# Head sums behind the first value product, division and factor sums moved into the next even step

## The chip, the cores and the metric

The kernel runs on one core of one Trainium2 chip, as one program with one launch. The metric is the device time in microseconds (us). TensorE does the matmuls and has a separate record for the loading of its stationary operand ("weight load", PEld in the profile). VectorE (DVE), ScalarE (ACT) and GpSimd (POOL) do the elementwise work, SyncE (SP) issues most transfers. Each engine works through its own queue in order, and waits on semaphores for the others.

## The reference

The input x has 4 sequences of 512 rows with 512 features. It is normalised, and the result is x plus an attention plus a mixture of expert networks, both of the normalised rows. All is float32. The change touches the attention alone. Its core, cut:

```python
scores = jnp.einsum('bhqd,bhkd->bhqk', q, k)          # 16 heads; 128 + 64 (rotary) features
scores = jnp.clip(scores, -80.0, 80.0)
causal = pos[:, None] >= pos[None, :]
scores = jnp.where(causal[None, None], scores, -jnp.inf)
weights = jax.nn.softmax(scores / jnp.sqrt(jnp.float32(d_qk)), axis=-1)
attn = jnp.einsum('bhqk,bhkd->bhqd', weights, v)
out = attn.transpose(0, 2, 1, 3).reshape(B, S, H * D_H) @ W_O.T
```

The softmax is split up in the kernel: exponentials first, the product with the values with them, and the division by their sum only on the product's result. No maximum is taken, since the clip bounds the scores.

## The kernel before

The first half of the program (to about 657 us) normalises, routes the rows and runs the experts; the experts' results lie in device memory (`y_d`), to be added later. The second half is the attention, a loop over 32 steps; step i works on one pair of heads of one sequence (4 sequences times 8 pairs). Everything in it is float32.

In step i:

- `scores` makes the scores of both heads of pair i in TensorE: eight matmuls from the plain features (L1432) and eight from the rotary ones (L1443). They lie in PSUM banks named a0, a1 (key block 0), c and a rotating one (block 2), b0 and b1 (blocks 1 and 3).
- `weights` lets VectorE clip them out of PSUM into `pt` (L1461, six operations), ScalarE take the exponentials (L1465), and GpSimd zero the upper triangles (L1469, eight masks). GpSimd then adds up the exponentials over the key blocks into `su`, one tile per head (L1493, L1497). A clip is what frees a score bank.
- For pair i + 1, TensorE makes the queries (L1282, L1297); VectorE turns the rotary ones with five operations (L1268, L1271), and GpSimd ends that with a subtraction (L1272). In the code this is `turn_q`.
- `values(i - 1, j)` multiplies the previous pair's exponentials with the values (L1513), and ScalarE copies the result into `og`, one tile for two pairs, that is for four heads.

Two pairs, four heads, form a group q, closed in an even step. The group's division has these parts:

- `sums(q)`: four matmuls of `su` with ones, 32 columns each, into one bank, and that bank is a0, the one that the scores use as well (L1532). VectorE takes the reciprocal `rc` (L1534).
- `spread_by_dma(q, rc)`: 16 small transfers on SyncE's queue copy the rows of `rc` to all partitions (`rb`, L1544).
- `divide(q)`: four VectorE multiplications of `og` by `rb` (L1566), then four additions and subtractions (L1572, L1575) that make the left factors for a Strassen-like product of seven block products instead of eight.
- `project_out(q)`: the seven block products with the output weights (L230, 56 matmuls) in banks b1, c and b0. ScalarE copies some results out (L1605), GpSimd adds these to the accumulator `acc` (L1612), and VectorE adds the rest straight from the banks (L1615, three operations; the last two free b0 and b1). In between `combine` adds the experts' rows of one of 16 row groups to `acc` with three VectorE operations (L1677), and `fetch` gathers the next three tiles of such rows by indirect transfers that GpSimd issues (L1664).

`project_out(q - 1)` is called in the even step after the one that made `sums(q - 1)`. So before the change the sums of group q come in even step i = 2q + 2, the division of group q in the odd step i + 1, and its projection in the even step i + 2.

Most instructions are recorded with `keep`, which holds them in the program's order on their engine. The indirect transfers and the GpSimd additions between them are placed by the scheduler.

Of the kernel before, what the change touches and what calls it, by code (L numbers as in the profile page):

```python
# [10 lines left out]
F32 = mybir.dt.float32  # L11
# [7 lines left out]
P = 128  # L19
B, S, D = 4, 512, 512  # L20
# [22 lines left out]
def kernel(  # L43
# [164 lines left out]
    def first_factors(add, sub, a11, a12, a21, a22, s1, s2, s4, s3):  # L208
        add(s1, a21, a22)
        sub(s2, s1, a11)  # L210
        sub(s4, a12, s2)
        sub(s3, a11, a21)
        return a11, a12, s4, a22, s1, s2, s3
# [998 lines left out]
    def lat(b, i):  # L1212
        return xnT[:, i, ts(b, S)]

    def project(b, psum):

        if b % 2 == 0:
            two = psum(f"pj_kr_{b}")
            for c in range(DC):
                for j in range(2):  # L1220
                    r = slice(j * DHR, (j + 1) * DHR)
                    keep(
                        nc.tensor.matmul(
                            two[r, :],
                            krT[:, c, r],
                            xnT[:, c, ts(b + j, S)],
                            start=(c == 0),
                            stop=(c == DC - 1),
                        )
                    )  # L1230
            raw = hw.tile([P, S], F32, tag="raw", name=f"kraw_{b}")
            keep(nc.scalar.copy(raw, two))
            turned[b] = hw.tile([P, S], F32, tag="kr", name=f"kr_{b}", bufs=1)
            rope(turned[b], raw, f"k{b}")
        ps = []
        for wT, name in ((dqT, "cq"), (dkvT, "ckv")):
            p = psum(f"pj_{name}_{b}")
            for c in range(DC):
                keep(
                    nc.tensor.matmul(  # L1240
                        p, wT[:, c, :], xnT[:, c, ts(b, S)], start=(c == 0), stop=(c == DC - 1)
                    )
                )
            ps.append(p)
        keep(nc.scalar.copy(lat(b, 0), ps[0]))
        keep(nc.vector.tensor_copy(lat(b, 1), ps[1]))

        src = turned[b - b % 2][(b % 2) * DHR : (b % 2 + 1) * DHR, :]
        for j in range(2):
            keep(nc.vector.tensor_copy(lat(b, 2)[j * DHR : (j + 1) * DHR, :], src))  # L1250
# [29 lines left out]
    def rotary_query(i, ps):  # L1280
        b, hp = pairs[i]
        keep(nc.tensor.matmul(ps, qrT[:, hp, :], lat(b, 0), start=True, stop=True))  # L1282
        raw = hw.tile([P, S], F32, tag="raw", name=f"qraw_{i}")
        qr = hw.tile([P, S], F32, tag="qr", name=f"qr_{i}", bufs=1)
        qs[i] = [qr]

        def copy():
            keep(nc.scalar.copy(raw, ps))

        def turn():  # L1290
            rope(qr, raw, f"q{i}")

        return copy, turn

    def query(i, j, ps):
        b, hp = pairs[i]
        keep(nc.tensor.matmul(ps, a_h[:, 2 * hp + j, :], lat(b, 0), start=True, stop=True))  # L1297
        qc = hw.tile([P, S], F32, tag=f"qc{j}", name=f"qc_{i}_{j}", bufs=1)
        qs[i].append(qc)

        def copy():
            keep(nc.scalar.copy(qc, ps))

        return copy
# [96 lines left out]
    ap = ctx.enter_context(tc.tile_pool(name="ap", bufs=2))  # L1401
# [4 lines left out]
    def psum(name):  # L1406
        return ps_p.tile([P, S], F32, tag="pj", name=name)
# [6 lines left out]
    def scores(i):  # L1414
        b = pairs[i][0]
        qr, *qc = qs.pop(i)
        bank = {}
        for j in range(2):
            bank[j, 0] = ps_s.tile([P, S], F32, tag=f"a{j}", name=f"sa_{i}_{j}")
            bank[j, 1] = bank[j, 3] = ps_s.tile([P, S], F32, tag=f"b{j}", name=f"sb_{i}_{j}")  # L1420
        bank[0, 2] = ps_s.tile([P, S], F32, tag="c", name=f"sc_{i}")
        bank[1, 2] = psum(f"sd_{i}")

        def where(j, kc):
            o = 3 * P if kc == 3 else 0
            return bank[j, kc][:, o : o + PT_W[kc]]

        order = [(j, kc) for kc in (0, 2, 1, 3) for j in range(2)]
        for j, kc in order:

            keep(
                nc.tensor.matmul(  # L1432
                    where(j, kc),
                    lat(b, 1)[:, ts(kc, P)],
                    qc[j][:, kc * P :],
                    start=(kc != 3),
                    stop=False,
                )
            )
        for j, kc in order:  # L1440
            r = slice(j * DHR, (j + 1) * DHR)
            keep(
                nc.tensor.matmul(  # L1443
                    where(j, kc),
                    lat(b, 2)[r, ts(kc, P)],
                    qr[r, kc * P :],
                    start=False,
                    stop=(kc != 1),
                )
            )  # L1450
        return bank
# [54 lines left out]
    def values(i, j):  # L1506

        b, q = pairs[i][0], i // 2
        pt = pts[i]
        av = psum(f"av_{i}_{j}")  # L1510
        for kc in range(TPB):
            keep(
                nc.tensor.matmul(  # L1513
                    av[:, kc * P :],
                    lat(b, 3)[:, ts(kc, P)],
                    pt[:, PT[j, kc] : PT[j, kc] + PT_W[kc]],
                    start=(kc == 0),
                    stop=(kc == TPB - 1),
                )
            )  # L1520
        if q not in og:
            og[q] = ap.tile([P, 4, S], F32, tag="og", name=f"og_{q}")
        keep(nc.scalar.copy(og[q][:, 2 * (i % 2) + j, :], av))

    def bank(tag):
        return lambda name: ps_s.tile([P, S], F32, tag=tag, name=name)

    def sums(q):

        sb = bank("a0")(f"sb_{q}")  # L1530
        for j, su in enumerate(sus.pop(2 * q) + sus.pop(2 * q + 1)):
            keep(nc.tensor.matmul(sb[ts(j, 32), :], ones[:, :32], su, start=True, stop=True))  # L1532
        rc = ap.tile([P, S], F32, tag="rc", name=f"rc_{q}", bufs=1)
        keep(nc.vector.reciprocal(rc, sb))  # L1534
        return rc
# [3 lines left out]
    def spread_by_dma(q, rc):  # L1539
        spread[q] = []  # L1540
        for j in range(4):
            rb = ap.tile([P, S], F32, tag="rb", name=f"rb_{q}_{j}", bufs=4)
            for m in range(4):
                nc.sync.dma_start(rb[ts(m, 32), :], rc[ts(j, 32), :])  # L1544
            spread[q].append(rb)
# [11 lines left out]
    def divide(q):  # L1557

        o = og.pop(q)

        for cols in half if q == n // 2 - 1 else [slice(0, S)]:
            for j, rb in enumerate(spread[q]):
                keep(nc.vector.tensor_mul(o[:, j, cols], o[:, j, cols], rb[:, cols]))  # L1566
        a11, a21 = (o[:, 0:2, half[t]] for t in range(2))
        a12, a22 = (o[:, 2:4, half[t]] for t in range(2))
        x = [ap.tile([P, 2, S // 2], F32, tag=f"s{k}", name=f"s{k}_{q}") for k in (1, 2, 4)]

        def add(*t):
            keep(nc.vector.tensor_add(*t))  # L1572

        def sub(*t):
            keep(nc.vector.tensor_sub(*t))  # L1575

        firsts_of[q] = first_factors(add, sub, a11, a12, a21, a22, *x, a21)
# [109 lines left out]
    for i in range(n):  # L1687
        more = i + 1 < n
        even = i % 2 == 0
        q = i // 2 - 1  # L1690
        held = scores(i)
        raw_copy, turn_q = rotary_query(i + 1, psum(f"pqr_{i + 1}")) if more else (nothing, nothing)
        qc_copy = query(i + 1, 0, psum(f"pq_{i + 1}_0")) if more else nothing
        weights(i, held, raw_copy, nothing if even else turn_q)
        qc_copy()
        if even and i > 0:
            spread_by_dma(q, sums(q))
        if even:
            turn_q()
        if i > 0:  # L1700
            values(i - 1, 0)
        if more:
            query(i + 1, 1, psum(f"pq_{i + 1}_1"))()
        if i < 2:
            project(2 + i, psum)
        if 1 < i < 5:
            turn_keys((2, 3, 1)[i - 2], psum)
        if i > 0:
            values(i - 1, 1)
        if even and i > 2:  # L1710
            project_out(q - 1, first_added=lambda: combine(q))
        if i == 1:
            combine(0)
        if even and i != 2 or i == 1:
            fetch((i + 1) // 2)
        if not even and i > 1:
            divide(q)

    q = n // 2 - 1

# [59 lines left out]
```

## Time and profile before

| | |
|---|---|
| median of 14 runs | 1340.21 us (1339.92 to 1341.24) |
| the profiled execution | 1340.78 us |
| its span, first to last instruction | 1339.0 us |
| busy: TensorE / weight loads / VectorE / ScalarE / GpSimd | 99 / 74 / 73 / 30 / 63% of the span |
| mean granted TensorE clock | 0.999 |
| first score matmul of step 0, step 31 | 657.39 us, 1291.85 us |
| reciprocal L1534 | 16 times, 3.35 us each |
| division's multiplications L1566 | 68 times, 68.6 us in all, median 0.77 us |
| clips L1461 into the rows of `sa` | 64 times, 0.68 us each |
| masks L1469 | 256 times, 0.57 us each on average |

A line of the timeline gives the start in us from the span's start, the busy time of the merged group in us, engine, source line, operation, output and input by name, shapes and count; in square brackets stands how long the engine was idle before it and what ended that. A line of the waits gives the waiting engine, tile and line, what released it, the total in us, how many times, and the longest. Matmuls overlap, so a group's start-to-next-start distance says more than its busy time. Each float32 matmul appears as two records.

### The profile page before, as it was taken

The numbers are of one execution on the slowest core, as the hardware profiler recorded it, in microseconds if no ns is written. First come the engines' busy times: TensorE is split into PE (matmuls) and PEld (weight loads), VectorE is DVE, ScalarE is ACT, GpSimd is POOL, SyncE is SP. The second block draws the span as 40 slices with busy tenths as digits, with TensorE's granted clock in tenths as the row PEclk, the third lists the DMA queues.
The fourth block names the chain that finished last, engine by engine and source line by source line (L and its number), as shares of the span: only waits on it lengthen the run. The fifth ranks groups of instructions, "written<-read, shape, count | busy, mean of one in ns | idle before, by whom it ended". The sixth has DMA issues, their size and how long they took to land.

```text
span 1339.0 us, 17913 instructions
## 1 busy us (share of the span) xinstructions
PE 1329.6 (99%) x5949; PEld 992.7 (74%) x5949; DVE 971.6 (73%) x1426; ACT 406.3 (30%) x714; POOL 847.7 (63%) x952
## 2 busy tenths in 40 slices
PE   9999999999999999999999999999999999999998
PEld 8778888888888888877655666666666666666676
DVE  7669486676767677676458679877788777897775
ACT  3333222322223322212223423323333323233231
POOL 5113664564545465532277789888898888988883
PEclk9999999999999999999999999999999999999999
DMA  8850355766567675533401331243322333213332
GB/s 280 192 158 19 92 134 159 219 180 185 185 169 204 164 228 162 156 92 99 142 21 46 111 109 37 85 132 110 110 56 73 124 111 110 82 53 118 110 110 87
DMA packets 174100, 167.90 MB, mean 125 GB/s; under 512 B 57904, under 2 KB 136752, under 8 KB 174000
## 3 DMA queue, kind: packets, MB, share of 16 engines
q1 hardware_dynamic: 161264, 133.10, 33.9%
q0 software_dynamic: 12736, 33.57, 8.6%
q8 instruction: 49, 0.80, 0.3%
q14 instruction: 51, 0.42, 0.1%
HBM read 116.02 MB, written 34.87 MB: 113 GB/s over the span
## 4 chain that ended last, share of the span: by engine, by line
PE 96%; DVE 2%; DMA 1%; SPq 1%; ACT 1%; issue 0%; POOL 0%; DVEq 0%; ACTq 0%; POOLq 0%
PE op L230 14%; PE av L1513 11%; PE yr L230 11%; PE hr L230 10%; PE gr L230 9%; PE sb L1432 4%; PE sa L1432 4%; PE pq L1297 4%; PE gs L230 3%; PE sa L1443 3%; PE ys L230 2%; PE pqr L1282 2%; PE hs L230 2%; PE sb L1443 2%; PE sb L1532 2%; PE h_s L142 1%
## 5 line engine op out<-in xcount | busy, mean ns | idle before, releaser
L182 POOL DMA_INDIRECT xs<-xn_d,idx_i x208 | 230.0, 1106 | 193.6 <-DVE xT L199 134.6
L1469 POOL TENSOR_TENSOR pt<-pt,tri 128x128 f32<-128x128 f32 x256 | 140.1, 567 | 68.4 <-ACT pt L1465 61.7
L1465 ACT ACTIVATE pt<-pt 128x512 f32<-128x512 f32 x160 | 94.4, 628 | 257.6 <-DVE pt L1461 256.6
L1513 PEld LDWEIGHTS av<-pt,xnT 128*128 128x128 f32 x512 | 95.4, 190 | 83.7 <-issue 47.7
L1513 PE MATMUL av<-pt,xnT 128*128 128x512 f32 (+3 forms) x512 | 149.8, 436 | 0.0
L230 PE MATMUL op<-m,og 128*128 128x256 f32 x512 | 118.6, 379 | 0.5 <-DVE og L1566 0.5
L1271 DVE TENSOR_TENSOR swap_q<-qraw,sinT 32x512 f32<-32x512 f32 x128 | 117.7, 919 | 1.7
L1497 POOL TENSOR_TENSOR su<-su,pt 128x256 f32<-128x256 f32 (+1 forms) x128 | 105.2, 822 | 10.0
L230 PEld LDWEIGHTS op<-m,og 128*128 128x128 f32 x512 | 96.0, 190 | 14.5 <-DVE og L1566 1.3
L1461 DVE TENSOR_SCALAR pt<-sa 128x512 f32<-128x512 f32 x64 | 41.1, 682 | 70.2 <-PE sa L1443 70.2
L1664 POOL DMA_INDIRECT yg<-y_d,pos_i x48 | 54.5, 1134 | 57.1 <-issue 50.2
L230 PE MATMUL op<-m,s 128*128 128x256 f32 x384 | 88.2, 379 | 0.1
L1497 POOL TENSOR_TENSOR su<-pt 128x384 f32<-128x384 f32 x64 | 83.8, 1310 | 0.0
L1612 POOL TENSOR_TENSOR acc<-acc,v 128x512 f32<-128x512 f32 x60 | 80.6, 1344 | 5.1 <-ACT v L1605 3.2
L230 PEld LDWEIGHTS op<-m,s 128*128 128x128 f32 x384 | 72.9, 190 | 10.3 <-issue 0.5
L1677 DVE SCALAR_TENSOR_TENSOR acc<-yg,wk,acc 128x512 f32<-128x512 f32 x48 | 56.7, 1181 | 19.1 <-POOL acc L1612 17.9
L1605 ACT COPY v<-op 128x512 f32<-128x512 f32 x64 | 37.5, 587 | 108.3 <-PE op L230 107.1
L1566 DVE TENSOR_TENSOR og<-og,rb 128x512 f32<-128x512 f32 (+1 forms) x68 | 68.6, 1069 | 0.6 <-PE rb L1552 0.2
L230 PE MATMUL yr<-w,at_r 128*128 128x256 f32 x288 | 67.1, 380 | 0.7 <-DVE at_r L351 0.4
L1615 DVE TENSOR_TENSOR acc<-op,acc 128x512 f32<-128x512 f32 x48 | 31.7, 687 | 49.5 <-POOL acc L1612 47.3
L230 PE MATMUL hr<-xT,w 128*128 128x256 f32 x288 | 66.1, 379 | 0.0
L230 PE MATMUL gr<-xT,w 128*128 128x256 f32 x288 | 66.1, 379 | 0.0
(339 smaller groups left out, 2809.2 us busy)
## 6 DMA issues: line engine op xcount, KB each, us to landing
m<-m_d SPq DMA_DIRECT2D x112, 256.0 KB
w<-in_L_ffn_W_dram SPq DMA_DIRECT2D x52, 512.0 KB
rb<-rc SPq DMA_DIRECT2D x240, 64.0 KB
w<-in_L_ffn_Wg_dram SPq DMA_DIRECT2D x26, 512.0 KB
y_d<-v_yr SPq DMA_DIRECT2D x36, 256.0 KB
y_d<-none SPq DMA_DIRECT2D x24, 256.0 KB
acc<-in_L_attn_x_dram SPq DMA_DIRECT2D x16, 256.0 KB
xn_d<-xp SPq DMA_DIRECT2D x16, 256.0 KB
```

The costliest lines, as they stand in the source:

```text
L182: nc.gpsimd.indirect_dma_start(out=xs[blk][:, q, :], out_offset=None, in_=xn_d[:, :], in_offset=bass.IndirectOffsetOnAxis(ap=idx_i[:, q, b ...
L230: nc.tensor.matmul(banks[k][:, t, :], a[p][:, j, ts(t, P)], b[p][:, j, :], start=(k not in used), stop=(t == j == 1), skip_group_check=True,)
L1271: keep(nc.vector.tensor_mul(swap[there, :], raw[here, :], tables[1][here, :]))
L1432: nc.tensor.matmul(where(j, kc), lat(b, 1)[:, ts(kc, P)], qc[j][:, kc * P :], start=(kc != 3), stop=False,)
L1443: nc.tensor.matmul(where(j, kc), lat(b, 2)[r, ts(kc, P)], qr[r, kc * P :], start=False, stop=(kc != 1),)
L1465: keep(nc.scalar.activation(t, t, AF.Exp, scale=QK_SCALE))
L1469: keep(nc.gpsimd.tensor_mul(m, m, tri))
L1497: nc.gpsimd.tensor_add(t[:, kc * P :], prev, pt[:, PT[j, kc] : PT[j, kc] + PT_W[kc]])
L1513: nc.tensor.matmul(av[:, kc * P :], lat(b, 3)[:, ts(kc, P)], pt[:, PT[j, kc] : PT[j, kc] + PT_W[kc]], start=(kc == 0), stop=(kc == TPB - 1),)
L1566: keep(nc.vector.tensor_mul(o[:, j, cols], o[:, j, cols], rb[:, cols]))
L1612: keep(eng.tensor_add(block, block, v))
L1677: nc.vector.scalar_tensor_tensor(acc[:, g, :], yg, wk[:, g, k : k + 1], acc[:, g, :], ALU.mult, ALU.add)
```

## The change

Three places of the attention loop change.

1. In an even step, `spread_by_dma(q, sums(q))` is called after `values(i - 1, 0)` instead of before it. On TensorE the four sum matmuls move behind eight value records; on VectorE the reciprocal moves behind the turn of the queries, since `turn_q` is called before.
2. `divide` is no longer called at the end of the odd step. Group q - 1 is divided in the next even step, behind the clips of `weights` and ahead of the turn; `project_out(q - 1)` follows later in the same step. The group left over at the end of the loop is divided right after it, which is the place where it was divided before.
3. The three tiles of the factor sums (`s1`, `s2`, `s4`) have one buffer each instead of two.

```diff
-        x = [ap.tile([P, 2, S // 2], F32, tag=f"s{k}", name=f"s{k}_{q}") for k in (1, 2, 4)]
+        x = []
+        for k in (1, 2, 4):
+            x.append(ap.tile([P, 2, S // 2], F32, tag=f"s{k}", name=f"s{k}_{q}", bufs=1))
...
         weights(i, held, raw_copy, nothing if even else turn_q)
         qc_copy()
-        if even and i > 0:
-            spread_by_dma(q, sums(q))
+        if even and i > 2:
+            divide(q - 1)
         if even:
             turn_q()
         if i > 0:
             values(i - 1, 0)
+        if even and i > 0:
+            spread_by_dma(q, sums(q))
         if more:
...
-        if not even and i > 1:
-            divide(q)
+    divide(q)
```

In the program's order VectorE's queue in an even step becomes: six clips, four multiplications and four factor sums of the division, five operations of the turn, the reciprocal, one bank addition, three operations of the combine, two bank additions. In an odd step it holds six clips and five operations of the turn. GpSimd's queue keeps its operations; in most even steps its second `acc` addition now stands ahead of the first two gather issues, in steps 4, 12, 20 and 28 it stands behind them, as it did before in every even step.

## The prediction

> **What bounds it now.** I read the busy shares, then the chain, then what the weight loads wait for (TensorE's own rows name no such wait), then the timeline of a pair of steps. The page:
>
> ```profile
> PE 1329.6 (99%) x5949; PEld 992.7 (74%) x5949; DVE 971.6 (73%) x1426; ACT 406.3 (30%) x714; POOL 847.7 (63%) x952
> ...
> PE 96%; DVE 2%; DMA 1%; SPq 1%; ACT 1%; issue 0%; POOL 0%; DVEq 0%; ACTq 0%; POOLq 0%
> ```
>
> TensorE is the chain. But a busy matmul row can hide a weight load that waits. The waits of the weight loads, 720 to 1290 us:
>
> ```profile
> PEld sb L1532 <- DVE pt L1461: 10.7, 14, 0.8
> PEld sb L1532 <- POOL su L1497: 4.4, 13, 0.4
> ```
>
> So the sums of four heads (L1532) come too early in each even step: their bank a0 is freed by a clip that stands behind the division, and the fourth `su` is late on GpSimd. The price is in TensorE's timeline; step 12 first, then the last sums, where nothing is late:
>
> ```profile
> 901.62 1.53 PE L1532 MATMUL sb<-su,ones 128*32 128x512 f32 x8
> 903.08 2.42 PE L1513 MATMUL av<-pt,xnT 128*128 128x512 f32 x8
> ...
> 923.03 1.90 PE L1432 MATMUL sb<-qc,xnT 128*128 128x384 f32 x8
> ```
> ```profile
> 1314.35 1.07 PE L1532 MATMUL sb<-su,ones 128*32 128x512 f32 x8
> ...
> 1315.35 1.99 PE L230 MATMUL op<-m,og 128*128 128x256 f32 x8
> ```
>
> From start to next start the sums take 1.46 us in step 12 and 1.00 at the end. By the first score matmuls (851.56, 879.18, 892.94, 920.45 ...) an even step lasts 27.51 us and an odd one 13.76, from step 5 to the end. VectorE and GpSimd in step 12 (one answer for each engine), where the combine waits for GpSimd's first addition:
>
> ```profile
> 900.86 1.28 DVE L1461 TENSOR_SCALAR pt<-sa 128x512 f32<-128x512 f32 x2
> ...
> 903.91 3.35 DVE L1534 RECIPROCAL rc<-sb 128x512 f32<-128x512 f32 x1
> 907.17 0.81 DVE L1268 TENSOR_TENSOR qr<-qraw,cosT 128x512 f32<-128x512 f32 x1
> 907.99 4.08 DVE L1271 TENSOR_TENSOR swap_q<-qraw,sinT 32x512 f32<-32x512 f32 x4
> 912.10 0.69 DVE L1615 TENSOR_TENSOR acc<-op,acc 128x512 f32<-128x512 f32 x1
> 915.68 2.33 DVE L1677 SCALAR_TENSOR_TENSOR acc<-yg,wk,acc 128x512 f32<-128x512 f32 x3 [2.88 <-POOL acc L1612]
> 920.82 1.29 DVE L1615 TENSOR_TENSOR acc<-op,acc 128x512 f32<-128x512 f32 x2 [2.82 <-POOL acc L1612]
> ```
> ```profile
> 914.38 1.27 POOL L1612 TENSOR_TENSOR acc<-acc,v 128x512 f32<-128x512 f32 x1
> 916.71 1.47 POOL L1664 DMA_INDIRECT yg<-y_d,pos_i  x1 [1.06 <-DVE acc L1677]
> 918.48 1.01 POOL L1664 DMA_INDIRECT yg<-y_d,pos_i  x1 [0.30 <-issue]
> 919.51 1.27 POOL L1612 TENSOR_TENSOR acc<-acc,v 128x512 f32<-128x512 f32 x1
> ```
>
> The last two additions free banks b0 and b1; the score matmul at 923.03 writes b0. VectorE has 1.5 us in hand there and 5.7 us of waits before, but no more. And step 31, the one place where the division already stands straight behind the clips:
>
> ```profile
> 1297.42 1.29 DVE L1461 TENSOR_SCALAR pt<-sa 128x512 f32<-128x512 f32 x2 [4.02 <-PE sa L1443]
> ...
> 1300.49 3.27 DVE L1566 TENSOR_TENSOR og<-og,rb 128x512 f32<-128x512 f32 x4
> ...
> 1306.13 1.48 DVE L1575 TENSOR_TENSOR og<-og 128x512 f32<-128x512 f32 x1
> ```
>
> **Sums behind the values.** No instruction is added. The clips now start when the scores are done, the fourth `su` has 2 us more, and the sums should take 1.00 us in place of 1.46. Step 4 has no such wait today (736.45 to 737.46). Saved: 0.46 x 13 even steps (6 to 30) = 6.0 us. Bounds: 0 if `su` stays late, 0.6 at most. The `su` buffers and a0 are held about 2 us longer; GpSimd's next `su` comes after its eight masks, later than that, so I price this at nothing.
>
> **Division into the even step.** Eight VectorE operations leave the odd step, where they take 8.5 us (851.09 to 859.59) and VectorE then has room, and enter the even step. I count from the first score matmul (0). Clips start at 5.57, the division at 8.64 and ends at 15.76 (step 31: 1291.85, 1297.42, 1300.49, 1307.61). The projection needs its first input at about 15 and s2 at about 18.7, so it doesn't wait.
>
> The five operations of the turn follow. The nearest row is 4.9 us (907.17 to 912.07); beside masks it was 4.5. GpSimd has 3.0 us of `su` work left at that point (0.59 + 0.45 + 0.29 + 0.99 + 0.72, step 31's rows), and the two engines alternate: a mask lasts 0.455 alone and 0.90 beside these operations, one each 0.86, so a VectorE operation holds GpSimd for 0.41. 3.0 + 5 x 0.41 = 5.1; it ends at 20.9. The reciprocal, now behind the turn, takes 3.26: 24.1. Bank addition 0.65: 24.8.
>
> Ten steps (6, 8, 10, 14, ...): the combine touches other rows than GpSimd's first addition and goes on at once. In step 10 it took 4.38 (three GpSimd operations beside it), alone 2.33; with two beside it I take 4.1: 28.9. Then 0.69 and 0.61: b0 free at 29.6, b1 at 30.2. The score matmuls want them at 27.51 - 0.46 + 2.58 = 29.63 and 30.28. That is no margin at all: I take 0.1 us of wait per step, between 0 and 0.5. 1.0 us.
>
> Four steps (4, 12, 20, 28; the combine's group lies in the block of the first addition): combine waits for that addition, GpSimd's second addition stands behind two gather issues that wait for the combine, and VectorE's last two additions wait for the second one. From the bank addition 0.14 + 1.27 to the end of the first addition: 26.2. From there 915.65 to 921.51 = 5.87 to the first of the last additions: b0 free at 32.1, wanted at 29.63 (step 4: 30.1). Wait 2.5, with 0.1 for the weight load behind it 2.6, in step 4 2.1. 3 x 2.6 + 2.1 = 9.9 us, between 6.5 (turn at 4.5) and 12. In the other ten GpSimd's queue has the second addition ahead of the gathers.
>
> Step 2 has no division, yet its reciprocal also goes behind the turn: 8.8 + 4.5 + 3.35 = 16.6, and step 3's first score matmul, which takes a0, starts at 15.39. 1.2 us (0.9 to 1.4).
>
> The rest: the 16 `rb` transfers a step start some 10 us later on SyncE's queue, with the factor loads behind them ending their issue near 39; both are used 15 us later or more: nothing. The one buffer in place of two for the factor sums: their readers in TensorE are a cycle back: nothing. GpSimd's last addition ends near 35, when the next masks start: nothing. After the loop all stands where it did.
>
> Sum: -6.0 + 1.0 + 9.9 + 1.2 = +6.1 us. The profiled execution took 1340.78 (span 1339.0 and 1.8 around it), 0.57 above the median 1340.21: it would be 1346.9, and the median 1346.3.
>
> The Trainium skill, SBUF — State Buffer, "Who interferes with whom", has VectorE and GpSimd exclude each other for a whole instruction. This trace shows only 0.41 of a VectorE operation's 0.69. By the page's rule the 13 operations would end 13 x 0.28 = 3.6 us later, 14 even steps would wait that much more and the time be near 1397. TensorE: Matmul & The Clock Gate ("What's actually happening") adds that about 3.4 us of idle TensorE halves its clock; the waits above stay below that, the granted clock here is 1.00 in all stretches, and no row shows what a longer wait does.
>
> **Rivals.**
> (1) Faster. The division and the turn run lighter, since GpSimd finishes `su` earlier. Alone, a VectorE operation is 0.69 with 0.61 between starts: 13 x 0.61 ends the turn at 16.6, b0 is free before 29.6 in all 14 steps, step 2 loses nothing: 1340.2 - 6.0 = 1334. It decides once the last bank addition comes 2.6 us earlier than I count. Against it: GpSimd's 7 us of masks and `su` lie just there.
> (2) Level. The four steps lose 1.7, the ten nothing: -6.0 + 6.5 + 0.9 = +1.4: 1341.6.
> (3) Much slower. The division takes 8.5 as in the odd steps today and the combine 4.38: 1.7 us later everywhere: -6 + 10 x 1.8 + 9.9 + 4 x 1.7 + 1.4 = +30: 1370. Against it: the 8.5 had other GpSimd work beside it, and that work is done only once.
>
> **How the numbers follow.** Forecast 0.52 (own range 1343 to 1352), (1) 0.14, (2) 0.17, (3) 0.17. A measurement here tells 0.2%, 2.7 us, from no change. Faster: 0.14, rival 1's. Same: 0.16, nearly all of rival 2. Slower: 0.70, the rest. Range 1339 to 1354: it leaves out rival 1 and the upper part of rival 3.
>
> **What would show it.** Right: the sums about 1.0 us with no wait on a clip or `su`; no `og` operation in odd steps; waits of `sb` L1432 on VectorE's last additions, 2 us or more in four steps and under 0.5 in ten; step 3 starting 16.6 after step 2. Wrong: even-to-even pairs of 40.8 in all steps, or waits in all of them.

## The result, and the profile after

The changed kernel takes 1359.05 us (median of 6 runs, 1357.48 to 1360.64) against 1340.30 beside it (28 runs, 1339.92 to 1341.66): ratio 1.0139, 95% interval 1.0129 to 1.0149. It is 18.75 us slower. The forecast of 1346.3 had the direction, but not the size: the time lies 5 us above its range. The profiled execution took 1360.31 us, with a span of 1358.5, 19.5 us over the span before.

Four lines of the changed kernel's page: busy time, granted clock, chain, and the row of the scores that write b0 and b1.

```profile
PE 1332.4 (98%) x5949; PEld 994.4 (73%) x5949; DVE 960.6 (71%) x1426; ACT 405.8 (30%) x714; POOL 842.7 (62%) x952
...
PEclk9999999999999999999999999999999999999999
...
PE 70%; DVE 22%; issue 6%; POOL 1%; ACT 1%; DMA 0%; DVEq 0%; SPq 0%; POOLq 0%; ACTq 0%
...
L1432 PE MATMUL sb<-qc,xnT 128*128 128x384 f32 (+1 forms) x256 | 64.9, 399 | 15.2 <-DVE acc L1617 15.2
```

TensorE held 96% of the chain; now VectorE has 22% of it, and the `sb` scores wait for VectorE's last additions, a wait that the row of before did not have. The weight loads say how often (total, times, longest; 720 to 1320 us):

```profile
PEld sb L1432 <- DVE acc L1617: 25.0, 28, 3.4
```

The steps, from first score matmul to first score matmul, in the two traces:

| steps | before | after | difference |
|---|---|---|---|
| 2 and 3 | 15.39 + 14.20 | 16.58 + 14.30 | +1.3 |
| 13 even steps, 6 to 30 | 357.7 (27.52 each) | 351.5 (27.04 each) | -6.2 |
| nine odd steps, 7, 9, 11, 15, 17, 19, 23, 25, 27 | 123.8 (13.76 each) | 129.4 (14.38 each) | +5.6 |
| odd steps 5, 13, 21, 29 | 55.0 | 18.24, 17.03, 18.67, 18.66 | +17.6 |
| behind the start of step 31 | 47.16 | 48.03 | +0.87 |

With 0.4 for a start 0.4 us later, that is the 19.5, but for rounding. The change does what it says in the even steps and loses three times as much in the odd ones. TensorE's timeline of the changed kernel: the sums of step 10 and the scores of step 11, then the stalls of steps 13 and 21.

```profile
868.88 1.06 PE L1532 MATMUL sb<-su,ones 128*32 128x512 f32 x8
869.87 1.13 PE L1297 MATMUL pq<-xnT,a_h 128*128 128x512 f32 x2
...
888.17 2.00 PE L1432 MATMUL sb<-qc,xnT 128*128 128x384 f32 x8 [0.35 <-DVE acc L1617]
...
928.64 0.59 PE L1432 MATMUL sd<-qc,xnT 128*128 128x256 f32 x2
932.25 2.00 PE L1432 MATMUL sb<-qc,xnT 128*128 128x384 f32 x8 [3.00 <-DVE acc L1617]
...
1096.97 0.59 PE L1432 MATMUL sd<-qc,xnT 128*128 128x256 f32 x2
1100.59 3.28 PE L1432 MATMUL sb<-qc,xnT 128*128 128x384 f32 x8 [3.02 <-DVE acc L1617]
1103.80 1.49 PE L1443 MATMUL sa<-qr,xnT 64*128 64x512 f32 x4
```

The sums take 0.99 us and wait for nothing. The wait in step 11 is short, and the ones in steps 13 and 21 are 3.0 us long; but in step 21 the matmuls behind the wait are slow as well, 3.28 us for eight that took 2.00 in step 13. The windows of the same kernel show why (us; busy time of each engine; granted clock, PEclk; share of the DMA engines):

```profile
core 0: us, PE busy (x) PEld busy (x) DVE busy (x) ACT busy (x) POOL busy (x), PEclk, DMA share, GB/s
...
926.00:937.00 11.00, 8.00 (x37) 4.76 (x36) 5.21 (x9) 0.88 (x2) 7.76 (x8) 1.00 0.62 162
1094.00:1105.00 11.00, 7.98 (x25) 4.76 (x25) 3.54 (x5) 0.00 (x0) 7.93 (x7) 0.84 0.67 178
```

The granted clock is 1.00 around the stall of step 13 and 0.84 around that of step 21: 0.16 x 11 us is 1.8 us of clock lost, which at half speed takes 3.5 us. Steps 5 and 29 show the same (0.84 and 0.85). A step with it is 18.67 us, one without 17.03: 1.64 us each. The page's row of 40 slices is too coarse to see it. Narrower windows show the stretch exactly, and what stands ahead of it (columns as above):

```profile
930.48:933.89 3.41, 1.65 (x7) 1.08 (x8) 1.29 (x2) 0.00 (x0) 3.24 (x3) 1.00 0.83 246
933.89:937.30 3.41, 3.41 (x22) 2.11 (x21) 1.96 (x5) 1.17 (x2) 1.72 (x2) 1.00 0.73 183
1097.73:1101.14 3.41, 0.55 (x2) 0.30 (x2) 1.29 (x2) 0.00 (x0) 3.27 (x3) 1.00 0.80 218
1101.14:1104.56 3.42, 3.42 (x10) 2.22 (x10) 0.00 (x0) 0.00 (x0) 2.28 (x2) 0.50 0.79 202
```

The borders are those at which the trace lets the clock change, all whole multiples of 3.413 us apart. TensorE was busy for 0.55 us in the window ahead of the halved one; the stall of step 13 was spread over two windows, and in the emptier one TensorE was still busy for 1.65 us.

VectorE in step 10, which started at 858.04:

```profile
866.79 3.52 DVE L1566 TENSOR_TENSOR og<-og,rb 128x512 f32<-128x512 f32 x4
...
871.93 1.37 DVE L1577 TENSOR_TENSOR s<-og,s 128x512 f32<-128x512 f32 x1
873.23 1.21 DVE L1577 TENSOR_TENSOR og<-og 128x512 f32<-128x512 f32 x1
874.36 0.94 DVE L1268 TENSOR_TENSOR qr<-qraw,cosT 128x512 f32<-128x512 f32 x1
875.31 4.08 DVE L1271 TENSOR_TENSOR swap_q<-qraw,sinT 32x512 f32<-32x512 f32 x4
879.43 3.36 DVE L1534 RECIPROCAL rc<-sb 128x512 f32<-128x512 f32 x1
882.82 0.69 DVE L1617 TENSOR_TENSOR acc<-op,acc 128x512 f32<-128x512 f32 x1
883.43 4.09 DVE L1679 SCALAR_TENSOR_TENSOR acc<-yg,wk,acc 128x512 f32<-128x512 f32 x3
887.44 1.28 DVE L1617 TENSOR_TENSOR acc<-op,acc 128x512 f32<-128x512 f32 x2
```

From the clips to the last addition VectorE has no idle time: its own work in the even step has become the chain. GpSimd in step 20, where the combine's group lies in the block of the first addition:

```profile
1093.41 1.27 POOL L1614 TENSOR_TENSOR acc<-acc,v 128x512 f32<-128x512 f32 x1 [2.91 <-DVE acc L1617]
1095.73 1.47 POOL L1666 DMA_INDIRECT yg<-y_d,pos_i  x1 [1.06 <-DVE acc L1679]
1097.50 1.01 POOL L1666 DMA_INDIRECT yg<-y_d,pos_i  x1 [0.30 <-issue]
1098.54 2.49 POOL L1614 TENSOR_TENSOR acc<-acc,v 128x512 f32<-128x512 f32 x2
```

The second addition starts 5.1 us after the first, behind two gather issues, and VectorE's last additions wait for it until 1099.84.

### The profile page after: what moved, and what is told of

Same layout as the page of the kernel before. It is cut to its first block, busy times and chain, and to the rows that moved or that the text cites. A ratio compares the mean times of both kernels' runs of the same rounds, so it can differ in the third digit from the quotient of the medians.

```text
span 1358.5 us, 17928 instructions
## 1 busy us (share of the span) xinstructions
PE 1332.4 (98%) x5949; PEld 994.4 (73%) x5949; DVE 960.6 (71%) x1426; ACT 405.8 (30%) x714; POOL 842.7 (62%) x952
## 4 chain that ended last, share of the span: by engine, by line
PE 70%; DVE 22%; issue 6%; POOL 1%; ACT 1%; DMA 0%; DVEq 0%; SPq 0%; POOLq 0%; ACTq 0%
PE yr L230 10%; PE hr L230 10%; PE gr L230 10%; PE av L1513 5%; PE sb L1432 5%; DVE rc L1534 4%; DVE og L1566 4%; DVE swap_q L1271 3%; PE sa L1443 3%; PE gs L230 3%; DVE pt L1461 3%; PE ys L230 2%; PE hs L230 2%; PE sa L1432 2%; PE pq L1297 2%
## 5 line engine op out<-in xcount | busy, mean ns | idle before, releaser
L1469 POOL TENSOR_TENSOR pt<-pt,tri 128x128 f32<-128x128 f32 x256 | 166.5, 673 | 46.9 <-ACT pt L1465 42.3
L230 PE MATMUL op<-m,og 128*128 128x256 f32 x512 | 118.7, 380 | 0.5 <-DVE og L1566 0.5
L1614 POOL TENSOR_TENSOR acc<-acc,v 128x512 f32<-128x512 f32 x60 | 83.7, 1406 | 44.8 <-DVE acc L1617 40.8
L230 PEld LDWEIGHTS op<-m,og 128*128 128x128 f32 x512 | 96.0, 190 | 14.7 <-DVE og L1566 1.3
L1497 POOL TENSOR_TENSOR su<-su,pt 128x256 f32<-128x256 f32 (+1 forms) x128 | 95.6, 747 | 10.0
L230 PE MATMUL op<-m,s 128*128 128x256 f32 x384 | 88.2, 379 | 0.1
L230 PEld LDWEIGHTS op<-m,s 128*128 128x128 f32 x384 | 72.9, 190 | 10.3 <-issue 0.5
L1432 PE MATMUL sb<-qc,xnT 128*128 128x384 f32 (+1 forms) x256 | 64.9, 399 | 15.2 <-DVE acc L1617 15.2
L1497 POOL TENSOR_TENSOR su<-pt 128x384 f32<-128x384 f32 x64 | 76.8, 1200 | 0.0
L1432 PEld LDWEIGHTS sb<-qc,xnT 128*128 128x128 f32 x256 | 43.6, 197 | 40.0 <-DVE acc L1617 25.0
L230 PE MATMUL yr<-w,at_r 128*128 128x256 f32 x288 | 66.9, 380 | 0.3
L1297 PE MATMUL pq<-xnT,a_h 128*128 128x512 f32 x128 | 66.6, 605 | 0.0
L230 PE MATMUL hr<-xT,w 128*128 128x256 f32 x288 | 66.1, 379 | 0.0
L230 PE MATMUL gr<-xT,w 128*128 128x256 f32 x288 | 66.1, 379 | 0.0
```

The source lines that it names most:

```text
L230: nc.tensor.matmul(banks[k][:, t, :], a[p][:, j, ts(t, P)], b[p][:, j, :], start=(k not in used), stop=(t == j == 1), skip_group_check=True,)
L1432: nc.tensor.matmul(where(j, kc), lat(b, 1)[:, ts(kc, P)], qc[j][:, kc * P :], start=(kc != 3), stop=False,)
L1469: keep(nc.gpsimd.tensor_mul(m, m, tri))
L1497: nc.gpsimd.tensor_add(t[:, kc * P :], prev, pt[:, PT[j, kc] : PT[j, kc] + PT_W[kc]])
L1614: keep(eng.tensor_add(block, block, v))
```

## The experiments

Times are read in two ways: the whole time against the kernel before on the same chip, and the stretch from the start of step 0 to the start of step 31, called the loop here (634.5 before, 652.7 after). The first four kernels ran on a chip where the program took some 50 us longer ahead of step 0, the kernel before too (1394.35 us); these four are therefore compared by their loop and what lies behind it.

**The division alone.** Sums and reciprocal go back ahead of the division and the turn; the division stays in the even step.

```
+        if even and i > 0:
+            spread_by_dma(q, sums(q))
         if even and i > 2:
             divide(q - 1)
...
-        if even and i > 0:
-            spread_by_dma(q, sums(q))
```

> The division stays behind the clips of the next even step; the sums of four heads and their reciprocal go back ahead of it and of the turn, where they stood before the change. Theory (VectorE's chain in the even step, division, turn, reciprocal, bank addition, combine, last additions, frees bank b0 too late, in whatever order reciprocal and division stand): the chain is as long as in the changed kernel, so the pairs of steps stay as they are, waits of about 0.6 us in ten steps and 3 in four; only step 2 gets its 1.2 us back: 1359.05 - 1.2 = 1357.9 us, 1352 to 1361. Rival A (the later reciprocal is what hurts, and the division is harmless): no wait of the sb scores on the last additions, 1340 to 1343 us.

Measured: 1406.06 against 1394.35, ratio 1.0079 (1.0046 to 1.0112); the loop is 644.5, 10.1 over before and 8.2 under after. Even steps 27.68, the ten ordinary odd steps 13.76, the four others 15.69, step 2 15.39. Neither theory holds: the waits fell from 0.6 to 0 and from 3.3 to 1.9, so the order of the reciprocal matters. VectorE in step 12 of this kernel:

```profile
960.63 3.36 DVE L1534 RECIPROCAL rc<-sb 128x512 f32<-128x512 f32 x1 [1.17 <-PE sb L1532]
964.00 4.03 DVE L1566 TENSOR_TENSOR og<-og,rb 128x512 f32<-128x512 f32 x4
...
971.56 2.77 DVE L1271 TENSOR_TENSOR swap_q<-qraw,sinT 32x512 f32<-32x512 f32 x4
974.37 0.69 DVE L1617 TENSOR_TENSOR acc<-op,acc 128x512 f32<-128x512 f32 x1
```

The four `swap_q` operations of the turn take 2.77 us in place of 4.08. The reciprocal reads one operand from PSUM, and GpSimd's work isn't slowed beside it (`su` additions of 1.00 and 1.26 us, as against 1.44 and 1.92 beside the multiplications); GpSimd ends `su` at 968.34, before the turn starts at 970.86. The bank addition starts 23.6 us into the step in place of 24.8, though 1.2 us were spent waiting for the sums. The sums stand ahead of the values, where they wait again: the even steps are 27.68.

**The sums alone.** From the kernel before, only the line with the sums is moved behind `values(i - 1, 0)`; the division stays in the odd step.

> Only the sums of four heads and their reciprocal go behind the values of the last pair's first head; the division stays in the odd step. Theory: VectorE's clips still stand behind the division of the odd step, so the values' last piece waits for its clip in place of the sums, and nothing of the 0.46 us per step is won unless the clips come earlier: the value matmuls lose about 1.0 us in each of 13 steps, less the 0.46: 1340.3 + 13 x 0.5 + 1.2 (step 2) = 1348 us, 1344 to 1352. Rival B (the sums' saving stands alone and the division is not needed for it): 1340.3 - 6.0 + 1.2 = 1335.5 us.

Measured: 1410.50, ratio 1.0108 (1.0066 to 1.0151); the loop is 644.6, 10.1 over before. Even steps 28.13 to 28.25, step 2 16.58, all odd steps from 5 on 13.76. That is the theory, with 0.6 us per even step for its 0.5. So the saving isn't to be had without the other part: what was late are the clips behind the division, and the values now wait for them (TensorE in step 12 of this kernel).

```profile
967.56 2.42 PE L1513 MATMUL av<-pt,xnT 128*128 128x512 f32 x8 [0.83 <-DVE pt L1461]
969.91 1.06 PE L1532 MATMUL sb<-su,ones 128*32 128x512 f32 x8
```

**The combine in the odd step.** The changed kernel, with combine and gathers moved behind the odd step's values.

```
-            project_out(q - 1, first_added=lambda: combine(q))
+            project_out(q - 1)
...
+        if not even and i > 3:
+            combine(q)
...
+            fetch(q + 1)
```

> The changed kernel, but the combine of three gathered rows and the gather of the next three stand in the odd step, behind its values, in place of between the projection's additions in the even step (steps 4 to 30). Theory: VectorE's last additions are 4 us earlier and GpSimd's additions follow each other with no gather between, so no scores wait for b0, no stall reaches 1 us, and the granted clock stays at 1.00; what is left is the saving of 0.46 us in 13 steps and step 2's 1.2: 1340.3 - 6.0 + 1.2 = 1335.5 us, 1334 to 1338. Rival A (division and reciprocal are too late by themselves, the combine is not needed for the loss): waits of 0.5 us or more in all even steps, 1343 us or more.

Measured: 1400.60, ratio 1.0033 (1.0001 to 1.0066). All odd steps from 5 on are 13.76, the clock has no dip in the loop: with the combine out of the way the last additions come in time. But the even steps are 27.45, not 27.05, so the loop is 634.9, and the stretch behind step 31 is 52.1 in place of 47.2 (the clock halves once in it, from 1377.37 to 1380.78). A miss of 5.2 us in the loop, with a cause in GpSimd's queue (step 10 of this kernel), and in the sums in TensorE's:

```profile
907.45 1.08 POOL L1666 DMA_INDIRECT yg<-y_d,pos_i  x1
908.57 0.73 POOL L1497 TENSOR_TENSOR su<-su,pt 128x256 f32<-128x256 f32 x1
909.46 1.03 POOL L1666 DMA_INDIRECT yg<-y_d,pos_i  x1 [0.16 <-issue]
```
```profile
914.54 1.58 PE L1532 MATMUL sb<-su,ones 128*32 128x512 f32 x8
```

The gathers now stand between the `su` additions and make the last one late for the sums, 1.52 us to the next matmul in place of 0.99.

**The combine in the odd step in four steps only**, those where its group lies in the block of the first addition.

> As the kernel with the combine in the odd step, but only for steps 4, 12, 20 and 28, where the group that is combined lies in the block of GpSimd's first addition; the other ten even steps are those of the changed kernel. Theory: the four long stalls go and with them the halved clock; ten waits of 0.6 us and step 2 are left: 1340.3 + 1.2 + 10 x 0.15 - 3 x 0.46 = 1341.6 us, 1340 to 1344, granted clock 1.00 throughout. Rival C (the halved clock comes from something else in these steps): odd steps of 15 us or more remain there with the clock at 0.5, 1345 us or more.

Measured: 1399.77, ratio 1.0027 (0.9991 to 1.0063). Steps 5, 13, 21 and 29 are 13.76; six of the other odd steps are 14.38, and three, 14.03; the even steps behind the moved gathers are 27.43, the others 27.04. The loop is 635.7: 17.0 us of the 18.2 are gone with the combine of four steps. That is the four long stalls, the halved clock included.

**The clock.** The next four ran on a chip with the times of the first session (the kernel before: 1340.39). The changed kernel again, and with filler matmuls in the four long stalls:

```
+    nc.gpsimd.memset(zeros, 0.0)
...
+            if i % 8 == 5 and i > 4 and (j, kc) == (1, 2):
+                for _ in range(8):
+                    keep(nc.tensor.matmul(where(0, 2), zeros, qc[0][:, 2 * P :], start=False, stop=False))
```

> The changed kernel once more, beside the next three on one chip. From the first score matmul of step 0 to that of step 31 it took 652.7 us against 634.5 before the change. Theory: the same again, 650 to 653, 1.65 us for each of the four long stalls that the halved clock hits; ten odd steps of 14.4, four of 17.0 or 18.7 us. Rival: the granted clock stays at 1.00 here, then 647.7.

> The changed kernel, with eight extra matmuls in steps 5, 13, 21 and 29, between the score matmuls before and those that wait for b0: zero weights, 128x256, added into the bank of the sc scores (1.7 us of work by the 0.215 us between two sc matmuls, less than the wait of 3.0). The output is the same. Theory (the halved clock follows TensorE's idle time, about 3.4 us between issues): no 0.5 in the clock records, four odd steps of 17.0 us, and 652.7 - 3 x 1.65 = 647.7 us from step 0 to step 31 (1354.1 us in the first session's terms). Rival C (the clock falls for another reason than idle time): the same 18.7 us steps as without the extra matmuls, 652 or more.

Measured: 1358.59 (1357.27 to 1359.66; ratio 1.0130, 1.0113 to 1.0147) for the changed kernel and 1355.31 (1355.17 to 1356.15; ratio 1.0111, 1.0094 to 1.0128) with the fillers. In the changed kernel this time steps 5, 13 and 29 had the halved clock (18.23, 18.68, 18.67) and step 21 had not (17.05). With the fillers all four are 17.21, and the clock is 1.00 in all of them: TensorE with more to do is 3.3 us faster (the loop: 649.0 against 652.8). Step 20 to 21 with fillers, and the window around it:

```profile
1094.76 0.59 PE L1435 MATMUL sd<-qc,xnT 128*128 128x256 f32 x2
1095.19 3.62 PE L1445 MATMUL sc<-qc,zeros 128*128 128x256 f32 x16
1098.64 0.81 PE L1435 MATMUL sb<-qc,xnT 128*128 128x384 f32 x2
```
```profile
1092.00:1103.00 11.00, 11.00 (x53) 7.90 (x52) 4.92 (x8) 0.58 (x2) 7.74 (x7) 1.00 0.62 172
```

The expectation had the filler at 1.7 us; each matmul is two passes, so it is 3.45, a little longer than the wait: hence 17.21 and not 17.04. The halved clock comes from TensorE standing idle.

**Without `su`.** GpSimd's additions of the weights are left out, and the sums read a constant tile; the output is another.

```
-            keep(nc.gpsimd.tensor_copy(t[:, :P], pt[:, PT[j, 0] : PT[j, 0] + P]))
...
-            su.append(t)
+            su.append(su_const)
```

> The changed kernel without the eight GpSimd operations per step that add up the clipped and masked weights: the sums of four heads read a constant tile in their place, so this part of the computation is left out and the output is another. Theory (VectorE's division and turn are slow because GpSimd works beside them): the four s operations of the division and the five of the turn run unhindered, 1.3 + 1.6 us less, the bank addition comes some 2.9 us earlier, ten waits vanish, the four long ones fall from 3.0 to below 0.6, step 2 loses nothing, the sums don't wait: 634.5 - 6.0 + 4 x 0.3 = 629.7 us from step 0 to step 31, 628 to 632. Rival (VectorE's own work is too long for the even step): waits of 2 us or more stay in four steps, 640 or more.

Measured: 1336.94, ratio 0.9975 (0.9965 to 0.9985); the loop is 631.0. Ordinary odd steps 13.76, the four others 13.81 to 14.24, even steps 27.04, no halved clock; step 2 is still 16.58. VectorE in step 10:

```profile
864.87 0.69 DVE L1571 TENSOR_TENSOR s<-og,s 128x512 f32<-128x512 f32 x1
865.48 0.68 DVE L1571 TENSOR_TENSOR og<-og 128x512 f32<-128x512 f32 x1
...
866.78 2.77 DVE L1271 TENSOR_TENSOR swap_q<-qraw,sinT 32x512 f32<-32x512 f32 x4
```

1.37, 1.21 and 4.08 became 0.69, 0.68 and 2.77. So VectorE's length in the even step is in good part GpSimd's `su` beside it. In step 2 it is the masks that lie beside the turn, which this kernel keeps: the turn takes 4.4 us there (705.97 to 710.35), and six masks run from 705.47 to 709.79. The expectation there was wrong.

**The gathers between GpSimd's second and third addition**, the combine in the odd step, and the sums of step 2 at their old place.

```
+        if i == 2:
+            spread_by_dma(q, sums(q))
...
+            project_out(q - 1, first_added=lambda: fetch(q))
...
+        if not even and i > 3:
+            combine(q)
```

> The combine in the odd steps again, but the gathers of three rows stay in the even step, in GpSimd's queue between its second and third addition; in step 2 the sums of four heads go back ahead of the turn. Theory: with the combine and the gathers both in the odd step, the gathers stood between GpSimd's su additions and made the last su 0.4 us late for the sums in each even step (27.44 in place of 27.04); here they don't, the even steps are 27.05, the odd 13.76, step 2 15.39: 634.5 - 13 x 0.46 = 628.5 us from step 0 to step 31, 1334.3 in the first session's terms. Rival: the 0.4 us wait for su comes back without any stall in the odd steps, since su is late by GpSimd's own load and only the stalls of the changed kernel hid that; then even steps of 27.4 and 634 us.

(In this kernel `first_added` is called after the second addition.) Measured: 1340.64, ratio 1.0001 (0.9991 to 1.0010). The loop is as expected to 0.3 us: 628.2, even steps 27.04, odd 13.76, step 2 15.39. So the saving of the sums stands without any stall to help it. But 6.4 us went behind step 31, 53.5 in place of 47.2. VectorE there, then GpSimd:

```profile
1294.02 2.77 DVE L1678 SCALAR_TENSOR_TENSOR acc<-yg,wk,acc 128x512 f32<-128x512 f32 x3
1296.71 3.90 DVE L1566 TENSOR_TENSOR og<-og,rb 128x512 f32<-128x512 f32 x4
...
1313.65 2.33 DVE L1678 SCALAR_TENSOR_TENSOR acc<-yg,wk,acc 128x512 f32<-128x512 f32 x3 [8.32 <-POOL acc L1614]
```
```profile
1308.86 1.01 POOL L1666 DMA_INDIRECT yg<-y_d,pos_i  x1 [0.30 <-issue]
1309.89 3.73 POOL L1614 TENSOR_TENSOR acc<-acc,v 128x512 f32<-128x512 f32 x3
```

One combine stands ahead of the division behind the loop, and the last gathers ahead of GpSimd's last additions, on which the last combine and the last reciprocal wait. TensorE stands idle for that, and its clock is 0.50 from 1321.32 to 1324.74: the 16 matmuls of L230 there take 5.41 us, 3.72 before the change, so about 1.7 of the 6.4 us are the clock's.

**The last group's gathers out of that stretch.** Group 14 is gathered in step 29; in step 30 combine and gather stand where the changed kernel has them.

> As the kernel with the gathers between GpSimd's second and third addition and the combine in the odd steps, but the last group's gathers leave the stretch behind step 31: the gather of group 14 stands in step 29, its combine and the gather of group 15 in step 30, where the changed kernel has them. Theory (that kernel was 6.3 us shorter than before up to step 31 and lost 6.3 behind it, because the last combine stood ahead of the last division on VectorE and the last gathers ahead of GpSimd's last additions): 628.2 us from step 0 to step 31 as there, 48 behind it as in the changed kernel, so 1335.1 us, 1334 to 1337. Rival (the last stretch is long for another reason, the earlier arrival of step 31 for one): still 53 behind step 31, 1340.

Measured: 1335.20 (1335.02 to 1335.92), ratio 0.9964 (0.9950 to 0.9978), faster than both kernels: a loop of 628.2 and 48.2 behind it. TensorE holds 93% of its chain again, VectorE 2%.

**The gathers behind all additions**, the combine left between VectorE's additions.

> The changed kernel, but in GpSimd's queue the gathers stand behind all of the projection's additions, in every even step; the combine stays between VectorE's additions. Theory (the long stalls are GpSimd's second addition standing behind two gather issues that wait for the combine): the four odd steps become ordinary ones, 14.4, the clock stays at 1.00, 14 waits of 0.62 are left: 634.5 - 6.1 + 1.2 + 13 x 0.62 = 637.6 us from step 0 to step 31, and 1343 to 1345 us. Rival (the combine's wait for the first addition, and VectorE's own chain, are what is long there): four odd steps of 16 us or more, 643 or more.

Measured: 1351.87, ratio 1.0087 (1.0071 to 1.0102). Steps 13, 21 and 29 are 15.66, step 5 15.21, the ordinary ones 14.12 to 14.38; no halved clock in the loop. The loop is 640.8, and 52.7 behind it, where the last gathers stand ahead of GpSimd's masks (1302.75 to 1306.47) and the clock halves once (1313.38 to 1316.79). The theory was half right: the two gather issues are 1.4 of the 3.3 us, and 1.9 stay. GpSimd in step 12 of this kernel:

```profile
920.32 1.26 POOL L1614 TENSOR_TENSOR acc<-acc,v 128x512 f32<-128x512 f32 x1 [2.91 <-DVE acc L1617]
924.09 3.83 POOL L1614 TENSOR_TENSOR acc<-acc,v 128x512 f32<-128x512 f32 x3 [2.50 <-DVE acc L1678]
```

The second addition doesn't only stand behind the gathers; it writes the other half of the columns of the same row groups, the combine's among them, and waits for the combine itself.

**The reciprocal ahead of the turn**, the sums behind the values.

```
-        if even:
-            turn_q()
         if i > 0:
             values(i - 1, 0)
         if even and i > 0:
             spread_by_dma(q, sums(q))
+        if even:
+            turn_q()
```

> The changed kernel with the turn of the next query behind the reciprocal in the even steps, not ahead of it. Theory (the turn is slow because GpSimd's su additions run beside it, and the reciprocal isn't slowed by them, so behind the reciprocal the turn is 1.6 us or more shorter): ten waits vanish, the four long ones fall to about 1.9 us as with the sums at their old place, no halved clock, step 2 within 0.3 of before: 634.5 - 6.1 + 4 x 1.9 = 636.0 us from step 0 to step 31, 635 to 639 as the query's last step on GpSimd comes later; 1341 to 1345 us. Rival (five VectorE operations and a reciprocal take the same time in either order): the same waits as in the changed kernel, 650 to 653.

Measured: 1343.05, ratio 1.0019 (1.0010 to 1.0029). Ordinary odd steps 13.76, the four others 15.28 and 15.71 to 15.74, no halved clock; step 2 15.46, step 3 15.45; the loop is 637.0. As expected: the same instructions in another order are 16 us faster than the changed kernel. Step 3 loses 1.25, as the query's last step on GpSimd comes later there. In step 12 of this kernel:

```profile
910.36 3.34 DVE L1534 RECIPROCAL rc<-sb 128x512 f32<-128x512 f32 x1
913.63 0.62 DVE L1268 TENSOR_TENSOR qr<-qraw,cosT 128x512 f32<-128x512 f32 x1
914.26 2.78 DVE L1271 TENSOR_TENSOR swap_q<-qraw,sinT 32x512 f32<-32x512 f32 x4
```

## Why the prediction was right in direction and wrong in size

Its sum was -6.0 + 1.0 + 9.9 + 1.2 = +6.1. Term by term:

- **Sums behind the values, -6.0: right.** The even steps went from 27.52 to 27.04, 13 x 0.48 = 6.2. It needs the earlier clips, as the run with the sums alone shows (28.1), and an undisturbed `su`, as the combine in the odd step (27.45) beside the gathers between the additions (27.04) shows.
- **Step 2, 1.2: right** (16.58; 15.39 again with the sums at their old place). Step 3's 0.1 wasn't foreseen.
- **Ten ordinary steps, 0.1 each: wrong by 5.2 us.** They lost 0.62 each, 6.2 with step 31's. The step that failed is the end of the division, taken from step 31 as 15.76; in step 10 it is 16.4 (858.04 to 874.44). It starts 0.1 us later there, the four multiplications take 3.52 us and not 3.27, and the last two `s` operations 1.37 and 1.21 where step 31 had 0.69 and 1.48; GpSimd comes to `su` 0.5 us earlier than in step 31. The turn and the reciprocal took what was summed, 5.0 and 3.4, and the bank addition ended at 25.5, not 24.8. The text had said "no margin at all", and then took 0.1: with b0 free at 29.6 and wanted at 29.63, each tenth in the chain is paid ten times. The upper end given, 0.5, was too low as well.
- **Four special steps, 9.9: wrong by 7.7 us.** They lost 17.6. The clock has 4.9 of it: three of the four were followed by 3.41 us at half speed, 1.64 us each. The other 12.7 are the wait, 3.3 in three steps and 2.8 in step 5, where 2.6 and 2.1 were summed: the same 0.7 us of a late chain. As to the clock, the step that failed is to price at nothing a wait that stays below 3.4 us: the waits did stay below, 3.0 us and 2.6, and the clock fell after three of four. By the border found below, even the waits of 2.6 us that it summed were long enough to be hit.
- **The rest at nothing: nearly right.** 0.2 us behind step 31 beside its wait of 0.6, and 0.4 of a later start, which is no work of the change.

1.3 + 6.2 + 17.6 - 6.2 is 18.9, and with the 0.6 us of the last point the 19.5 of the spans; the profiled execution, with three halved clocks, is 1.3 us above its median. The mechanism was the one forecast; what was missing was 5.2 + 2.8 us of sizes and 4.9 of a mechanism that was dismissed.

The rivals: the first one, a light division and turn once GpSimd is done early, is what the kernel without `su` shows (1336.9; it said 1334), and against it stood what the text named, `su` lying just there. The second, with 1.7 us for the four steps and nothing for the ten, had both too low, and the third, with 1.8 us in each of the ten, three times too much there. The whole-instruction lock between VectorE and GpSimd, by which the time would have been near 1397, isn't what these runs show: the turn took 5.0 us beside `su` and 3.4 without, near the 0.41 us of hold for each operation. The Trainium skill, SBUF — State Buffer ("Who interferes with whom"), states the whole-instruction lock of VectorE's two-port modes; of `tensor_tensor`, the operation here, it says that it contends with GpSimd's reads.

## What to carry to other kernels

Before work is moved into a stretch, add up what the receiving engine does there to the last instruction that frees something; a margin near zero is not a small cost, but a cost that comes back in every round. If two engines slow each other, the order decides: put an operation that is not slowed (here a reciprocal out of PSUM) beside the other engine's long work, and the ones that are slowed behind it. A wait on the matmul engine of 2 us or more has to be priced with the slow matmuls that can stand behind it, and a GpSimd or DMA-issuing instruction that is moved is to be followed into the queue that it lands in, in the last round too.

## What the runs showed of the hardware

- TensorE's clock halves after a short wait. Eight long stalls of the changed kernel were profiled in two executions. TensorE was idle for 3.0 us in six of them and for 2.6 in the two of step 5 (8.41 busy of 11.00). Six were followed by 3.41 us at 0.5, step 5 both times; of the stalls of 3.0 us two weren't, step 13 in one execution and step 21 in the other, so it isn't the step.
- What decides can be read from the clock records of all thirteen traces. Every complete stretch at one clock is a whole multiple of 3.413 us long, so the clock is set window by window on a fixed grid of that length. In the attention, the program's last microseconds left aside, every window in which TensorE was busy for 1.53 us or less was followed by one at 0.5 (nine cases, six of them these stalls with 0.55 to 1.41 us), and none with 1.65 us or more was. The two stalls without it lay across a border of the grid: TensorE was busy for 2.18 and 1.65 us in the two windows of the one, 1.72 and 2.07 of the other. So a wait costs the clock by where it falls on the grid; an estimate from the borders is that 1.9 us of idle time within one window is enough (3.41 - 1.53). Ahead of the attention three windows with 1.43 to 1.46 us (in the kernels with the combine in the odd step) had no 0.5 behind them, so the border is not sharp. In the 12 stalls of three other kernels, with TensorE idle for 1.7 us or less, no window falls under 1.70 us, and the clock stayed at 1.00. That the changed kernel's times spread over 3.2 us and those with filled stalls over 1.0 fits this.
- The Trainium skill, TensorE: Matmul & The Clock Gate ("What's actually happening"), has the clock fall after an idle window of about 3.4 us. The window's length agrees with these traces (3.413 us), but TensorE need not be idle throughout it: up to 1.53 us of work in it did not keep the clock up.
- A VectorE operation of two SBUF inputs beside GpSimd's additions: 0.68 to 0.69 alone, 1.21 and 1.37 beside `su`; the reciprocal of a PSUM bank took 3.34 to 3.36 in all kernels, and GpSimd's `su` operations beside it took 1.00 and 1.26 (128x384, two smaller ones) as against 1.44 and 1.92 beside the turn.
